# Band attention on Trainium2: the softmax sums in three pieces, and PSUM banks handed out by a list

## The chip, the cores and the metric

The kernel runs on one core of a Trainium2 chip. The metric is the device time of one execution in microseconds (us), as the median of several runs; smaller is better. TensorE (PE in the profile) multiplies, with PEld as its weight loads, VectorE is DVE, ScalarE is ACT, GpSimd is POOL and the sync engine, which issues the transfers, is SP. PSUM is the memory that PE writes to, eight banks of 512 fp32 columns on 128 partitions; DVE and ACT read it, POOL does not here.

## What is computed

One block of a model on x of shape (2, 256, 128, 128): batch, time, frequency band, channel. It has three residual steps: attention over time with a causal mask, attention over the bands with a band mask, and a feed-forward layer. Each is fed by a layer norm. There are 4 heads of 32 channels.

```python
cm, bm = _causal_mask(256), _band_mask(128, 16)      # bm: |i - j| <= 16
xt = _ln(x).transpose(0, 2, 1, 3)
x = x + _mha(xt, t_wi, t_bi, t_wo, t_bo, 4, cm).transpose(0, 2, 1, 3)
x = x + _mha(_ln(x), f_wi, f_bi, f_wo, f_bo, 4, bm)
x = x + gelu(_ln(x) @ w1.T + b1) @ w2.T + b2

# in _mha, per head
scores = q @ k.T / sqrt(32) + mask
o = softmax(scores) @ v
```

The change concerns the second attention. A sequence has 128 bands, and a query sees only the keys that are at most 16 bands away. A query among the first 48 bands therefore sees keys of the first 64 alone, one among the last 48 sees keys of the last 64 alone, and only the 32 queries in the middle see keys of both halves.

## The kernel before, in words

The work is cut into groups of four sequences (512 tokens). There are 128 groups over time, then sixteen **runs**, each of eight groups over bands (class `OverBands`) and eight groups of the feed-forward layer on the same tokens. The loop in `run` makes one pass, here called an iteration n, per group, and does in it the scores of group n, the softmax and value product of group n-1, the output product of group n-2 and the projections of group n+1. Within a run the iterations of the band groups are called n = 0 to 7 here, and n = 8 is the first of the feed-forward groups.

Every engine works in the order in which this loop writes its instructions (class `InOrder` pins it). An instruction that waits holds back everything behind it on its engine. In a steady iteration of the bands the engines do this:

- **PE**: scores of n (32 products on tiles of 32 rows by 64 columns); the softmax sums of n-1; values by weights of n-1; output product of n-2; query, key and value projections of n+1. The sums are four products, one per head, of a matrix of ones with the weights `pf` (keys on the 128 rows, 512 queries as columns), so that each of a head's 32 output rows holds the sum of that head.
- **ACT**: four exponentials of n (`pf<-bank`); the reciprocal of the sums of n-1 as a logarithm (`ln<-bank`) and an exponential (`r<-ln`); the copies of query, key and value projections of n+1 (`qT`, `kT`, `v`).
- **DVE**: limit and mask of the last head's scores in place (`bank<-bank,band`), called the clamp here; layer norm and turning for group n+3 (four `xh`, one `z`); residual sum of n-2 (`x<-bank,x`); one step that refines the reciprocal of n-1 (`bank<-bank,r`, then `u<-bank,r`) and the division (`oT<-bank,u`). In the iterations 3, 4, 5 and 7 of a run, statistics of a later layer norm follow (`stats`, `mv`).
- **POOL**: for the iterations that follow statistics, the root of the variance (`rstd`), then the band mask on the weights of the first three heads of n (six `pf<-pf`).

A PSUM bank is a tile of the pool `ps`, and bank numbers are handed out in the order in which the loop asks, one after the other, modulo eight (`turn_of_bank`). `OverBands.weigh` asks ahead for the banks of the output product and the query projection (`path.held`, `follow`). In the part over time the banks are named by hand (`place`, `banks`). A product that writes a bank waits until the last reader of what stood there is done.

The profile gives all recorded operations one line, that of the helper, so groups are told apart by tile names; a PSUM tile is called `bank` throughout. An fp32 product of PE makes two records in the trace.

Of the kernel before, what the change touches and what calls it, by code (L numbers as in the profile page):

```python
# [34 lines left out]
LARGE = 1e20  # L35
EXP_SET = "natural_log_exp_and_others"
# [327 lines left out]

def by_tile(t):

    return t.rearrange("p (i t q) -> p i t q", i=NT, q=D)


class Group:  # L370
# [7 lines left out]
    def __init__(self, path, src, dst, before=None, store=None):  # L378
        self.path, self.src, self.dst = path, src, dst
        self.before, self.store = before, store  # L380

# [179 lines left out]
class Attention(Group):  # L561
    which = None
    swapped = ()
# [7 lines left out]
    def queries_keys(self):  # L571
        path = self.path
        wf = path.k.wf[self.which]
        self.qp = path.bank([P, NT * P], "qp", self.place.get("qp", path.held.pop("qp", None)))
        product(path, self.qp, wf[:, 0:P], self.xnT)

        self.kp = path.bank([P, NT * P], "kp", self.place.get("kp"))
        product(path, self.kp, wf[:, P : 2 * P], self.xnT)

    def take_query(self):  # L580
        path = self.path
        self.qT = path.work.tile([P, NT * P], F32, name="qT")
        path.scalar.activation(self.qT, self.qp, AF.Identity, bias=path.k.bq[self.which], scale=1.0)

    def take_key(self):
        path = self.path
        self.kT = path.work.tile([P, NT * P], F32, name="kT")
        path.scalar.copy(self.kT, self.kp)

    def values(self):  # L590
        path = self.path
        wv = path.k.wf[self.which][:, 2 * P : 3 * P]
        self.vp = path.bank([P, NT, P], "vp", self.place.get("vp"))
        for i in range(NT):
            product(path, self.vp[:, i], self.xnT[:, i * P : (i + 1) * P], wv, turn=2 if i in self.swapped else 0)

    def take_values(self):
        path = self.path
        self.v = path.work.tile([P, NT, P], F32, name="v", bufs=4)
        path.scalar.copy(self.v, self.vp)  # L600

# [13 lines left out]
    def divide(self):  # L615

        path, vector = self.path, self.path.vector
        if self.r0 is None:
            self.oT = path.work.tile([P, NT * P], F32, name="oT", bufs=2)
            u = path.work.tile([P, NT * P], F32, name="u", bufs=2)  # L620
            vector.tensor_tensor(by_rows(u), by_tile(self.op), by_tile(self.r), ALU.mult)
            vector.tensor_scalar(self.oT, u, -1.0, None, ALU.mult)
            return
        vector.tensor_tensor(self.rp, self.rp, self.r0, ALU.mult)
        u = path.work.tile([P, NT * P], F32, name="u", bufs=2)
        vector.scalar_tensor_tensor(u, self.rp, 2.0, self.r0, ALU.subtract, ALU.mult)
        self.oT = path.work.tile([P, NT * P], F32, name="oT", bufs=2)
        vector.tensor_tensor(by_rows(self.oT), by_tile(self.op), by_tile(u), ALU.mult)

    def output(self):  # L630
        path = self.path
        self.yp = path.bank([P, NT, P], "yp", self.place.get("yp", path.held.pop("yp", None)))
        for i in range(NT):
            product(path, self.yp[:, i], self.oT[:, i * P : (i + 1) * P], path.k.wn[self.which])

    def finish(self):
        self.path.vector.tensor_tensor(self.dst(), self.yp, self.dst(), ALU.add)
        if self.store is not None:
            self.store()
# [13 lines left out]
class OverTime(Attention):  # L653
# [7 lines left out]
    def values(self):  # L661
        path = self.path
        wv = path.k.wf[self.which][:, 2 * P : 3 * P]
        self.vp = [path.bank([P, 2, P], "vp", self.place.get(f"vp{s}")) for s in range(2)]
        for i in range(NT):
            product(
                path, self.vp[i // 2][:, i % 2], self.xnT[:, i * P : (i + 1) * P], wv, turn=2 if i in self.swapped else 0
            )

    def take_values(self):  # L670
        path = self.path
        self.v = path.work.tile([P, NT, P], F32, name="v", bufs=4)
        for s in range(2):
            path.scalar.copy(self.v[:, 2 * s : 2 * s + 2], self.vp[s])

    def first_tiles(self):
# [3 lines left out]
        self.s0 = {h: path.bank([P, 2, 2 * P], "sp", path.banks[f"a{h}"]) for h in range(H)}  # L680

    def second_tiles(self):
# [3 lines left out]
        self.s1 = {h: path.bank([P, 2, P], "sp", path.banks[f"b{h}"]) for h in range(H)}  # L686
# [15 lines left out]
    def first_weights(self, heads):  # L702
        for h in heads:
            self.path.scalar.activation(self.p0[:, :, h], self.s0[h], AF.Exp)

    def second_weights(self, heads):
        for h in heads:
            self.path.scalar.activation(self.p1[:, :, h, 0], self.s1[h], AF.Exp)

# [17 lines left out]
    def weigh(self):  # L727
        path, v = self.path, self.v
        rp = path.bank([P, 2, 2, P], "rp", self.place.get("rp"))
# [4 lines left out]
        op = path.bank([P, 2, 2 * P], "op", self.place.get("op"))  # L734
# [33 lines left out]
class OverBands(Attention):  # L768
# [3 lines left out]
    follow = ("yp",)  # L772
    by_vector = 1

    def scores(self, heads):
        path = self.path
        self.sp = {h: path.bank([P, NT * P], "sp") for h in heads}
# [12 lines left out]
    def first_function(self):  # L790
# [6 lines left out]
        for h in range(H):  # L797
            path.scalar.activation(self.p[:, h].rearrange("p i q -> p (i q)"), self.sp[h], AF.Exp)

# [13 lines left out]

    def weigh(self):
        path = self.path

        path.held = {name: path.turn_of_bank() for name in self.follow}
        self.rp = path.bank([P, NT * P], "rp")
        for h in range(H):
            path.tensor.matmul(  # L820
                self.rp[rows_of(h), :], path.k.ones[:, 0:D], self.p[:, h].rearrange("p i q -> p (i q)"),
                start=True, stop=True,
            )
        self.op = path.bank([P, NT * P], "op")
# [7 lines left out]
class FeedForward(Group):  # L832
# [8 lines left out]
    def hidden(self, js):  # L841
        path = self.path
        for j in js:
            self.hp[j] = path.bank([P, NT * P], "hp")
            product(path, self.hp[j], path.k.w1f[:, j * P : (j + 1) * P], self.xnT)

    def gelus(self, js):
        path = self.path
        for j in js:
# [3 lines left out]
            )  # L853

# [14 lines left out]
    def weigh(self):  # L869
        path, NI = self.path, self.path.k.NI  # L870
        if self.last:
            zp = [path.bank([P, P], "zp") for i in range(NT)]
        else:
            self.zp = path.bank([P, NT, P], "zp")
# [11 lines left out]
    def divide(self):  # L886
# [5 lines left out]
        else:  # L892
            self.path.vector.tensor_tensor(self.dst(), self.zp, self.dst(), ALU.add)
        self.store()
# [17 lines left out]
class BoundedPath:  # L912
    def __init__(self, ctx, tc, k):
# [6 lines left out]
        self.next_bank = 0  # L920
        self.inputs = 0
        self.held = {}
# [20 lines left out]
    def turn_of_bank(self):  # L943
        i, self.next_bank = self.next_bank, (self.next_bank + 1) % 8
        return i

    def bank(self, shape, name, i=None):

        flat = self.ps[self.turn_of_bank() if i is None else i][:, 0 : math.prod(shape[1:])]
# [224 lines left out]
    def verdict(self):  # L1174

        vector, C = self.vector, P
        tp = self.bank([P, 6], "tp")
# [97 lines left out]
    def run(self, x, out):  # L1275
# [15 lines left out]
        for i in range(len(groups) - 2):  # L1291
            if at(i, OverBands) and at(i + 1, OverBands):
                groups[i].follow = ("yp", "qp")

# [18 lines left out]
        for n in range(len(groups) + 2):  # L1313
# [6 lines left out]
            if n + 4 in early:  # L1320
                do(n + 4, "root")
            do(n, "first_half", "first_function", "first_mask")
# [73 lines left out]
            if not bands[2] and not turn:  # L1396
                statistics_of_feed(n)
            do(n - 1, "weigh")
# [26 lines left out]
            do_at(n + 1, OverBands, "queries_keys", "take_query", "take_key")  # L1425
# [15 lines left out]
            do_at(n + 1, OverBands, "values", "take_values")  # L1441
            if old is not None or new is not None:
# [70 lines left out]
```

## Time and profile before

| | before |
|---|---|
| median of 3 runs | 2633.57 us (2630.35 to 2633.73) |
| span of the profiled execution, first to last instruction | 2631.9 us |
| TensorE clock granted | 1.000 |
| PE busy | 2617.8 us, 99% |
| PE weight loads | 1837.4 us, 70% |
| DVE busy | 2140.8 us, 81% |
| ACT busy | 1838.8 us, 70% |
| POOL busy | 1958.6 us, 74% |

The span of the profiled execution lies 1.7 us under the median of the runs. The share of busy time is a mean over three different parts (time, bands, feed-forward). [...]

### The profile page before, as it was taken

The numbers are of one execution on the slowest core, as the hardware profiler recorded it, in microseconds if no ns is written. First come the engines' busy times: TensorE is split into PE (matmuls) and PEld (weight loads), VectorE is DVE, ScalarE is ACT, GpSimd is POOL, SyncE is SP. The second block draws the span as 40 slices with busy tenths as digits, with TensorE's granted clock in tenths as the row PEclk, the third lists the DMA queues.
The fourth block names the chain that finished last, engine by engine and source line by source line (L and its number), as shares of the span: only waits on it lengthen the run. The fifth ranks groups of instructions, "written<-read, shape, count | busy, mean of one in ns | idle before, by whom it ended". The sixth has DMA issues, their size and how long they took to land.

```text
span 2631.9 us, 156460 instructions
## 1 busy us (share of the span) xinstructions
PE 2617.8 (99%) x68688; PEld 1837.4 (70%) x68688; DVE 2140.8 (81%) x6410; ACT 1838.8 (70%) x3543; POOL 1958.6 (74%) x2311
## 2 busy tenths in 40 slices
PE   9999999999999999999999999999999999999999
PEld 6666666666766767666777776667676677777776
DVE  8888888888888887977878779788797797887974
ACT  7989988999899875564655746647557466475573
POOL 7999999999999987666667666665776666757762
PEclk9999999999999999999999999999999999999999
DMA  6656555565565454445454544554454445554543
GB/s 155 167 149 158 149 149 149 155 155 149 149 158 149 122 127 119 115 123 127 118 124 124 123 122 117 126 128 120 122 126 120 120 119 131 123 120 123 123 104 88
DMA packets 469797, 344.97 MB, mean 131 GB/s; under 512 B 43120, under 2 KB 404464, under 8 KB 469104
## 3 DMA queue, kind: packets, MB, share of 16 engines
q1 hardware_dynamic: 468408, 334.41, 50.5%
q8 instruction: 540, 8.85, 1.5%
q14 instruction: 153, 1.25, 0.2%
q10 hardware_dynamic: 696, 0.46, 0.1%
HBM read 167.98 MB, written 166.72 MB: 127 GB/s over the span
## 4 chain that ended last, share of the span: by engine, by line
PE 99%; DVE 0%; issue 0%; DMA 0%; ACT 0%; ACTq 0%; DVEq 0%
PE bank L907 99%; DMA x<-in_x 0%; DVE xh L907 0%; DVE bank L907 0%; DVE res L907 0%; DVE stats L907 0%; DVE oT L907 0%; DVE u L907 0%; DVE xnT L907 0%; ACTq L907 0%; ACT p L907 0%; DVE vy L907 0%; ACT lnv L907 0%; DVE mv L907 0%; ACT root L907 0%
## 5 line engine op out<-in xcount | busy, mean ns | idle before, releaser
L907 ACT ACTIVATE hT<-bank,b 128x512 f32<-128x512 f32 x512 | 348.1, 688 | 524.2 <-PE bank L907 483.2
L907 POOL TENSOR_SCALAR_AFFINE_SELECT pf<-pf 128x512 f32<-128x512 f32 x768 | 477.7, 637 | 185.3 <-ACT pf L907 159.1
L907 PEld LDWEIGHTS bank<-w2T_sb,hT 128*32 128x32 f32 x16384 | 467.4, 110 | 54.8 <-issue 29.0
L907 PE MATMUL bank<-xnT,wf 128*32 128x512 f32 x4096 | 492.4, 592 | 0.5 <-DVE xnT L907 0.5
L907 PE MATMUL bank<-xnT,w1f 128*32 128x512 f32 x4096 | 486.3, 592 | 0.2 <-issue 0.2
L907 PE MATMUL bank<-w2T_sb,hT 128*32 128x128 f32 x16384 | 482.8, 273 | 1.0 <-issue 1.0
L907 ACT ACTIVATE p<-bank 128x512 f32<-128x512 f32 (+1 forms) x1024 | 430.6, 494 | 62.9 <-PE bank L907 62.9
L907 DVE TENSOR_SCALAR xh<-x,mv,rstd 128x160 f32<-128x160 f32 (+1 forms) x1012 | 394.3, 432 | 59.7 <-POOL rstd L907 49.4
L907 POOL TENSOR_SCALAR_AFFINE_SELECT p<-p 128x1024 f32<-128x1024 f32 (+2 forms) x384 | 364.5, 949 | 57.5 <-ACT p L907 49.1
L907 PEld LDWEIGHTS bank<-wf,xnT 128*32 128x32 f32 x8192 | 243.3, 110 | 144.1 <-issue 101.6
L907 POOL TENSOR_TENSOR p<-p,p 128x512 f32<-128x512 f32 x256 | 324.6, 1291 | 10.6
L907 DVE BATCH_NORM_STATS2 stats<-x 128x6 f32<-128x128 f32 x1536 | 329.0, 276 | 3.4 <-DMA x<-in_x 3.4
L907 POOL TENSOR_SCALAR rstd<-mv 128x4 f32<-128x4 f32 x251 | 57.8, 230 | 361.7 <-DVE mv L907 360.5
L907 PEld LDWEIGHTS bank<-xnT,w1f 128*32 128x32 f32 x4096 | 183.6, 110 | 171.6 <-issue 109.6
L907 PE MATMUL bank<-qT,kT 32*64 32x80 f32 (+4 forms) x16384 | 302.0, 271 | 0.1
L907 PEld LDWEIGHTS bank<-qT,kT 32*64 32x64 f32 x16384 | 260.0, 131 | 51.2 <-ACT kT L907 50.6
L907 DVE TENSOR_TENSOR res<-bank,res 128x512 f32<-128x512 f32 (+1 forms) x259 | 170.3, 658 | 153.3 <-PE bank L907 144.7
L907 ACT ACTIVATE pf<-bank 128x512 f32<-128x512 f32 x512 | 265.8, 602 | 35.5 <-PE bank L907 31.3
L907 PE MATMUL bank<-wn,oT 128*32 128x128 f32 x8192 | 283.8, 274 | 0.1
L907 DVE STREAM_TRANSPOSE z<-xh 128x512 f32<-128x512 f32 x380 | 270.3, 711 | 13.3
L907 PE MATMUL bank<-wf,xnT 128*32 128x128 f32 x8192 | 276.5, 273 | 0.0
L907 POOL TENSOR_TENSOR rstd<-rstd,mhalf 128x4 f32<-128x4 f32 x251 | 260.8, 1039 | 20.9
(100 smaller groups left out, 3820.3 us busy)
## 6 DMA issues: line engine op xcount, KB each, us to landing
turned<-z SPq DMA_DIRECT2D x1520, 64.0 KB, 2.7
xnT<-turned SPq DMA_DIRECT2D x380, 256.0 KB, 3.2
x<-res SPq DMA_DIRECT2D x256, 128.0 KB, 2.5
x<-x SPq DMA_DIRECT2D x128, 256.0 KB, 4.1
out<-res SPq DMA_DIRECT2D x252, 128.0 KB, 2.3
x<-in_x SPq DMA_DIRECT2D x124, 256.0 KB, 4.3
x<-in_x SPq DMA_DIRECT2D x4, 128.0 KB, 2.8
x<-in_x SPq DMA_DIRECT2D x6, 64.0 KB, 2.9
```

What stands on the lines that cost most here:

```text
L907: return self.tc.keep_in_program_order(emit(*args, **kwargs))
```

## The change

The sums of a band group are made in three pieces where both neighbours in the loop are band groups (seven of the eight groups of a run, 112 of 128):

- `outer_sums`, right behind the scores of the next group: queries 0 to 47 of each sequence by keys 0 to 63, and queries 80 to 127 by keys 64 to 127. These are eight products on tiles of 64 rows by 32 columns and 192 columns long. The two halves write two banks, `rp` and `lower`.
- then the query projection of group n+1 and its copy, which were further down;
- then `middle_sums`: queries 48 to 79 by all 128 keys, four products of 128 columns into `rp`, and the values by weights as before.

ACT's logarithm becomes two (columns 0 to 79 of each sequence from `rp`, 80 to 127 from `lower`), and DVE's first refining product becomes two, of which one reads `lower` and writes into `rp`. Banks are now handed out by a list: `take` removes the first free one, `give` appends it once the code has written its last reader, and the order of the list is that of the giving.

```diff
+    def outer_sums(self):
+
+        self.split = True
+        self.rp = self.take("rp", [P, NT * P])
+        self.lower = self.take("lower", [P, NT * EDGE])
+        for h in range(H):
+            self.sums_of(h, in_tiles(self.rp)[:, :, 0:EDGE], slice(0, EDGE), slice(0, HALF))
+            self.sums_of(h, in_tiles(self.lower), slice(P - EDGE, P), slice(HALF, P))
+
+    def middle_sums(self):
+        q = slice(EDGE, P - EDGE)
+        for h in range(H):
+            self.sums_of(h, in_tiles(self.rp)[:, :, q], q, slice(0, P))
+
+    def sums_of(self, h, to, q, rows):
+        self.path.tensor.matmul(
+            to[rows_of(h)], self.path.k.ones[rows, 0:D], self.p[rows, h, :, q],
+            start=True, stop=True, skip_group_check=True,
+        )
...
+        path.scalar.activation(in_tiles(ln)[:, :, 0 : P - EDGE], in_tiles(self.rp)[:, :, 0 : P - EDGE], AF.Ln)
+        path.scalar.activation(in_tiles(ln)[:, :, P - EDGE : P], in_tiles(self.lower), AF.Ln)
...
+        vector.tensor_tensor(rp[:, :, low], in_tiles(self.lower), r0[:, :, low], ALU.mult)
+        self.give("lower")
+        vector.tensor_tensor(rp[:, :, q], rp[:, :, q], r0[:, :, q], ALU.mult)
...
     def weigh(self):
         path = self.path
 
-        path.held = {name: path.turn_of_bank() for name in self.follow}
-        self.rp = path.bank([P, NT * P], "rp")
-        for h in range(H):
-            path.tensor.matmul(
-                self.rp[rows_of(h), :], path.k.ones[:, 0:D], self.p[:, h].rearrange("p i q -> p (i q)"),
-                start=True, stop=True,
-            )
-        self.op = path.bank([P, NT * P], "op")
+        if self.split:
+            self.middle_sums()
...
+        self.op = self.take("op", [P, NT * P])
...
+            if bands[1] and bands[2]:
+                do(n - 1, "outer_sums")
+            if bands[2] and bands[3]:
+                do(n + 1, "queries", "take_query")
             do(n - 1, "weigh")
             do(n - 1, "invert_exactly" if turn else "invert")
...
-            do_at(n + 1, OverBands, "queries_keys", "take_query", "take_key")
+            if bands[2] and bands[3]:
+                do(n + 1, "keys", "take_key")
+                do_at(n - 1, OverBands, "give_sums")
+            else:
+                do_at(n - 1, OverBands, "give_sums", "give_values")
+                do_at(n + 1, OverBands, "queries_keys", "take_query", "take_key")
```

How the instructions move is shown at three places of a steady iteration of the bands. The first is PE, behind the last scores product of the iteration. Before:

```order
L907 MATMUL bank_114<-pf,ones 32x512 [waits Pool_49] x3
L907 MATMUL bank_114<-pf,ones 32x512
L907 MATMUL bank_115<-pf,v 32x128 [waits Activation_49]
L907 MATMUL bank_115<-pf,v 32x128 x15
L907 MATMUL bank_112<-wn_241,oT 32x128 [waits DVE_49]
L907 MATMUL bank_112<-wn_241,oT 32x128 x15
L907 MATMUL bank_113<-xnT,wf_238 32x512 [waits DMAHW6_49]
```

With the change, from the same place to the value product:

```order
L999 MATMUL bank_111<-pf,ones 32x4x48 [waits Pool_49]
L999 MATMUL bank_109<-pf,ones 32x192 [waits DVE_49]
L999 MATMUL bank_111<-pf,ones 32x4x48 [waits Pool_49]
L999 MATMUL bank_109<-pf,ones 32x192
L999 MATMUL bank_111<-pf,ones 32x4x48 [waits Pool_49]
L999 MATMUL bank_109<-pf,ones 32x192
L999 MATMUL bank_111<-pf,ones 32x4x48
L999 MATMUL bank_109<-pf,ones 32x192
L999 MATMUL bank_114<-xnT,wf_238 32x512 [waits DMAHW6_49,Activation_49]
L999 MATMUL bank_114<-xnT,wf_238 32x512 x3
L999 MATMUL bank_111<-pf,ones 32x4x32 x4
L999 MATMUL bank_108<-pf,v 32x128 [waits DVE_49]
```

Four long products became eight short ones, four query products and four middle ones. The first product into `lower` (bank 109 here) now waits for DVE, whose `u<-bank,r` of the group before read the same bank as that group's `rp`.

The second place is DVE between the residual sum and the statistics of one iteration. Before:

```order
L907 TENSOR_TENSOR x_33598<-bank_110,x_33598 128x512 [waits PE_49]
L907 TENSOR_TENSOR bank_112<-bank_112,r_35893 128x512 [waits Activation_49]
L907 SCALAR_TENSOR_TENSOR u<-bank_112,r_35893 128x512 [waits DVE_49]
L907 TENSOR_TENSOR oT<-bank_113,u 128x4x4x32 [waits DVE_49]
L907 BN_STATS stats<-x_33598 128x6 x4
```

With the change:

```order
L999 TENSOR_TENSOR x_34028<-bank_115,x_34028 128x512 [waits PE_49,Activation_49]
L999 TENSOR_TENSOR bank_110<-bank_113,r_36734 128x4x48 [waits Activation_49]
L999 TENSOR_TENSOR bank_110<-bank_110,r_36734 128x4x80 [waits DVE_49]
L999 SCALAR_TENSOR_TENSOR u<-bank_110,r_36734 128x512 [waits DVE_49]
L999 TENSOR_TENSOR oT<-bank_108,u 128x4x4x32 [waits DVE_49]
```

One product became two, and the second waits for the first one's result, since both write the same bank.

The third place is ACT, from the exponential of the last head on. Before:

```order
L907 ACTIVATE pf<-bank_113 128x512 [waits DVE_49]
L907 ACTIVATE ln<-bank_108 128x512 [waits PE_49]
L907 ACTIVATE r_36189<-ln 128x512 [waits Activation_49]
L907 ACTIVATE qT<-bank_115,bq_283 128x512 [waits PE_49]
L907 COPY kT<-bank_110 128x512 [waits PE_49]
```

With the change:

```order
L999 ACTIVATE pf<-bank_112 128x512 [waits DVE_49]
L999 ACTIVATE qT<-bank_114,bq_283 128x512 [waits PE_49]
L999 ACTIVATE ln<-bank_110 128x4x80 [waits PE_49]
L999 ACTIVATE ln<-bank_113 128x4x48
L999 ACTIVATE r_36734<-ln 128x512 [waits Activation_49]
L999 COPY kT<-bank_109 128x512 [waits PE_49]
```

The copy of the queries now stands ahead of the reciprocal. The banks of the scores also change hands: in a steady iteration the four of them are those that were read last by the exponential of the last head, the copy of the queries, the residual sum and the product on `lower` of the iteration before.

116 lines of the change are left out of this document (88 added, 28 removed).

## The prediction

> **What bounds the kernel now.** I read the chain of waits first, then the stretch of one undisturbed run of band groups (2201 to 2266 us) in order of time on PE, DVE and ACT, then the groups by shape for prices.
>
> ```profile
> PE 99%; DVE 0%; issue 0%; DMA 0%; ACT 0%; ACTq 0%; DVEq 0%
> ```
>
> By the chain, PE sets the end everywhere, and less work on PE should be less time. The order of time on PE in iteration 5 of that run (start, length, records), with the scores of iterations 1 to 3 and the output product of the run's last band group:
>
> ```profile
> 2208.67 0.96 PE L907 MATMUL bank<-qT,kT 32*64 32x80 f32 x64
> 2214.02 0.97 PE L907 MATMUL bank<-qT,kT 32*64 32x80 f32 x64
> 2220.25 0.96 PE L907 MATMUL bank<-qT,kT 32*64 32x80 f32 x64
> ...
> 2232.71 0.97 PE L907 MATMUL bank<-qT,kT 32*64 32x80 f32 x64
> 2233.60 1.07 PE L907 MATMUL bank<-pf,ones 128*32 128x512 f32 x8
> 2234.49 1.06 PE L907 MATMUL bank<-pf,v 128*32 128x128 f32 x32
> 2235.36 1.06 PE L907 MATMUL bank<-wn,oT 128*32 128x128 f32 x32
> 2236.23 1.90 PE L907 MATMUL bank<-xnT,wf 128*32 128x512 f32 x16
> 2237.95 1.06 PE L907 MATMUL bank<-wf,xnT 128*32 128x128 f32 x32
> 2238.93 0.96 PE L907 MATMUL bank<-qT,kT 32*64 32x80 f32 x64
> ...
> 2261.92 1.14 PE L907 MATMUL bank<-wn,oT 128*32 128x128 f32 x30
> ```
>
> From start to start the iteration is 6.22 us without a gap: scores 0.89, sums 0.89, values 0.87, output 0.87, query and key 1.72, value projection 0.98. DVE in the same run, from the clamp of iteration 3 to that output product, and its busy time in most of that stretch:
>
> ```profile
> 2221.40 0.70 DVE L907 SCALAR_TENSOR_TENSOR bank<-bank,band 128x512 f32<-128x512 f32 x1 [0.63 <-PE bank L907]
> ...
> 2224.28 0.65 DVE L907 TENSOR_TENSOR x<-bank,x 128x512 f32<-128x512 f32 x1
> 2224.86 0.69 DVE L907 TENSOR_TENSOR bank<-bank,r 128x512 f32<-128x512 f32 x1
> 2225.58 0.69 DVE L907 SCALAR_TENSOR_TENSOR u<-bank,r 128x512 f32<-128x512 f32 x1
> 2226.31 0.69 DVE L907 TENSOR_TENSOR oT<-bank,u 128x512 f32<-128x512 f32 x1
> 2226.91 0.86 DVE L907 BATCH_NORM_STATS2 stats<-x 128x6 f32<-128x128 f32 x4
> ...
> 2227.97 0.67 DVE L907 SCALAR_TENSOR_TENSOR bank<-bank,band 128x512 f32<-128x512 f32 x1
> ...
> 2254.66 1.61 DVE L907 TENSOR_SCALAR xh<-x,mv,rstd 128x160 f32<-128x160 f32 x4 [1.48 <-POOL rstd L907]
> ...
> 2261.44 0.43 DVE L907 TENSOR_SCALAR oT<-u 128x512 f32<-128x512 f32 x1
> ```
>
> ```profile
> 2221.40:2252.00 30.60, 29.90 (x74) 1.00 0.52 129
> ```
>
> This is what the chain does not tell. I call the time from the first scores product to the clamp the lag: 2221.40 less 2220.25 is 1.15 us, its least, since the clamp waits for the scores there. An iteration with statistics then takes DVE 6.57 (2221.40 to 2227.97), more than PE's 6.23, and the lag grows. From 2221.40 to 2252.00 DVE is busy for 29.90 of 30.60 us. It then waits 1.48 for a root that POOL makes of its own last statistics, goes through the reciprocal, and ends the division of the run's last group at 2261.44 + 0.43 = 2261.87. PE starts the product of that division at 2261.92, 0.05 later. So from iteration 3 of a run to that product **two engines are level**: time saved on PE gains nothing there, and time added on DVE arrives at 2261.92 in full.
>
> **The change on PE.** Sixteen records of 512 columns take 1.72 us with four tiles side by side: 0.43 per record, 0.84 ns per column. The outer sums have 192 columns, 0.16 per record and two records a tile: 0.32 if all eight tiles run side by side. A change of tile shape costs the 0.11 by which the value projection, before the scores, is longer than the value product of equal records (0.98 against 0.87). One such change is new, from 64 rows to 128; with 0.05 for first weights (an estimate, half of that 0.11) the outer sums take 0.48. The middle ones are eight records of 128 columns, a quarter of 0.87: 0.22. With 0.03 for the query's first weights it is 0.73 against 0.89, so **0.15 less** an iteration.
>
> No row shows a tile of 64 rows. The nearest are the scores over time, 64 records in 1.31 us (402.55 to 403.86) with 160 columns on average, 0.134 each: 6.5 run side by side there.
>
> ```profile
> 402.55 1.39 PE L907 MATMUL bank<-qT,kT 32*64 32x64 f32 x64
> 403.86 1.08 PE L907 MATMUL bank<-wn,oT 128*32 128x128 f32 x32
> ```
>
> If four at a time ran, the outer sums would be 0.80 and the iteration 0.17 longer. I take 0.15 less, by that row.
>
> ```profile
> L907 PE MATMUL bank<-p,v 128*32 128x256 f32 x2048 | 158.3, 379 | 1.3 <-issue 1.3
> L907 PE MATMUL bank<-p,ones 128*32 128x256 f32 x2048 | 134.0, 379 | 0.0
> L907 ACT ACTIVATE p<-bank 128x512 f32<-128x512 f32 x512 | 292.2, 597 | 0.6 <-PE bank L907 0.6
> L907 ACT ACTIVATE p<-bank 128x256 f32<-128x256 f32 x512 | 183.6, 390 | 62.3 <-PE bank L907 62.3
> L907 DVE TENSOR_TENSOR bank<-bank,r 128x512 f32<-128x512 f32 x240 | 166.8, 695 | 102.1 <-PE bank L907 78.9 <-ACT r L907 23.2
> L907 DVE TENSOR_TENSOR res<-bank,res 128x128 f32<-128x128 f32 x4 | 1.1, 291 | 3.7 <-PE bank L907 3.7
> ```
>
> The new sums write PSUM in runs of 48 and 32 columns. The time part's sums (`p,ones`) write two runs of 128 and take 379 ns, as long as `p,v`, which writes 256 columns in one run. The Trainium skill, page "PSUM — Partial Sum Buffer", section "Specifications (TRN2)", says that any non-contiguous access slows matmuls significantly; at runs of 128 this trace does not agree, and for shorter runs no row here shows it. I charge nothing in the sum and keep it as a rival.
>
> **The change on ACT and DVE.** ACT's price is 0.81 ns a column (207 ns for 256), so the logarithm's pieces of 320 and 192 columns are 0.44 and 0.34 long. An exponential passes on after 0.48 (row of four below, 1.93), 0.11 before its end: 0.33 + 0.37 against the 0.66 of one, **+0.04**. DVE's is 1.05 ns a column (695 against 291): pieces of 0.36 and 0.49. Each next one needs the one before, which costs 0.03 beyond the length (2224.86 to 2225.58 is 0.72 for 0.69). That is 0.39 + 0.52 against 0.72: **+0.19** for each split group. If the second piece did not wait for the first it would start 0.07 before its end (the residual sum, 0.65, passes on after 0.58): +0.09. With the fixed part of 0.16 and both waits in full it is +0.22. I take 0.19, since the order has the second piece wait.
>
> **Up to iteration 3.** ACT in iteration 1, with the refining step on DVE behind it:
>
> ```profile
> 2209.68 2.07 ACT L907 ACTIVATE pf<-bank 128x512 f32<-128x512 f32 x4 [0.29 <-PE bank L907]
> 2211.61 0.63 ACT L907 ACTIVATE ln<-bank 128x512 f32<-128x512 f32 x1
> 2212.27 0.63 ACT L907 ACTIVATE r<-ln 128x512 f32<-128x512 f32 x1
> 2212.80 0.67 ACT L907 ACTIVATE qT<-bank,bq 128x512 f32<-128x512 f32 x1
> 2213.38 0.57 ACT L907 COPY kT<-bank 128x512 f32<-128x512 f32 x1
> ...
> 2212.93 0.70 DVE L907 TENSOR_TENSOR bank<-bank,r 128x512 f32<-128x512 f32 x1 [0.16 <-ACT r L907]
> ```
>
> ACT runs through and ends `kT` at 2213.95, just before the scores at 2214.02, so ACT already sets iteration 1 (5.35), and PE's 0.15 is worth nothing in it; the split logarithm makes it 5.39. With the copy of the queries ahead, the reciprocal ends 0.58 + 0.04 later, and DVE, which waited for it (0.16), starts its product 4.88 us after the scores, not 4.26. Its `u` ends at 4.88 + 0.39 + 0.52 + 0.69 = 6.48. Behind it the first product into `lower` waits, and everything on PE behind that; PE would be there at 5.39 + 0.90 = 6.29. With 0.06 for the signal (estimate, near the 0.05 above) it loses 0.25, so iteration 2 is 6.23 - 0.15 + 0.25 = 6.33. **Scores of iteration 3: 0.14 later.**
>
> The lag: with the query product between, the output product ends, and with it the residual sum can start, at 0.90 + 0.48 + 0.89 + 0.22 + 0.87 + 1.06 + 0.10 = 4.52 after the scores (DVE comes there at 1.15 + 2.88 = 4.03 now, 2221.40 to 2224.28). In iteration 2 it is 4.77 with the stall. From there to the next clamp are 0.58 + 0.91 + 0.73 + 0.60 = 2.82, which gives 7.59 less 6.33: lag 1.26 at iteration 3, **0.11 more**. There DVE reaches the residual sum at 1.26 + 2.88 = 4.14 and waits to 4.52: **0.38 more**. After that the lag is so long that this wait is gone.
>
> **The sum.** Iterations 3 to 7 each hold one split product: 5 x 0.19 = 0.95. 0.14 + 0.11 + 0.38 + 0.95 = 1.58 us a run arrive at the run's last output product; sixteen runs give 25. PE pauses for instructions now and then, as in the first row, after which DVE's clamp waits for PE again (the second, two iterations on):
>
> ```profile
> 1599.81 0.64 PE L907 MATMUL bank<-pf,v 128*32 128x128 f32 x16 [0.30 <-issue]
> ...
> 1611.23 0.70 DVE L907 SCALAR_TENSOR_TENSOR bank<-bank,band 128x512 f32<-128x512 f32 x1 [0.33 <-PE bank L907]
> ```
>
> All its idle time is 14 us (2631.9 less 2617.8). Where DVE leads, such pauses cost nothing more; I estimate a fifth, 3 us, saved. So +22: 2631.9 becomes 2654, and with the 1.7 by which the median lies above the profile, **2655 us**. Where the wait shows: scores of n+1 need the bank that the product on `lower` reads, lag + 2.88 + 0.58 + 0.36 + 0.06 after the scores of n. That makes iterations of about 6.1, 6.2, 6.8 and 6.8 from 3 on, with lags of 2.3, 2.9, 2.9 and 1.8 (6.2 before). POOL's masks, which follow a root of DVE's statistics, are late by the same lag, and the first three heads' outer sums can wait for them too.
>
> **The rivals.**
>
> *The outer sums are slow* (tiles four at a time, or short runs in PSUM; the page's rule is this case). 0.32 more in iteration 2, in the wait of iteration 3 and some 0.1 in iteration 1: 0.75 a run more, 12 us, 2667. The row of 6.5 side by side speaks against the first, nothing against the second. Chance 0.13.
>
> *DVE's pieces are nearly free and the early waits hide in the lag.* 5 x 0.09 less the 3 us: +4, 2638. For it: DVE's rows overlap by 0.07 where none depends on another; against: the order has them wait. Chance 0.15.
>
> *PE is the bound after all, and it is faster.* In the run around 1600 us a pause let DVE catch up, and the clamp's wait of 0.33 shows PE leading there; if that holds for all, 0.15 in each of seven iterations and sixteen runs is 17 us: 2617. It decides from the point where DVE's additions in a run stay below its idle time there (0.7 of 30.6 us). I add twice as much. Chance 0.12.
>
> That the change does less than it says I exclude: the order shows 112 split groups with these shapes.
>
> **Numbers.** Forecast 0.60, rivals 0.13, 0.15 and 0.12. A measurement here tells about 0.2% (5 us) from no change. Faster 0.12; the second rival within 5 us and its edge, 0.14; slower 0.74. The range runs from 2634, just below the second rival, to 2672, above the first.
>
> **What would show it.** Right: in the profile after, scores starts 6.6 to 6.9 apart in iterations 5 and 6 of a run, lags above 2, DVE without idle time from iteration 3 to the last `oT`, two DVE pieces taking 0.9 together, `lower` waiting for DVE in iteration 2. Wrong: iterations of 6.1 throughout, a lag that returns to 1.15, or outer sums far from 0.48 from start to start.

## The result, and the profile after

The changed kernel takes 2668.85 us in the median (2664.89 to 2673.35, four runs) against 2632.64 of the kernel before (2630.35 to 2633.73, four runs). The ratio is 1.0138, with a 95% interval of 1.0125 to 1.0150: **36 us slower**. Forecast were 2655, in a range of 2634 to 2672.

The profiled execution of the changed kernel is 2673.35 us with a span of 2671.3, so it is the longest of the four, 39 us over the span before. Its chain of waits, as shares of the span by engine, is no longer PE alone:

```profile
PE 82%; DVE 11%; DMA 2%; ACT 2%; issue 2%; POOL 1%; SPq 1%; ACTq 0%; DVEq 0%; POOLq 0%
```

The order of time on PE in one run of band groups, that which starts at 1797 us (start, length, records): scores of iterations 1 to 3, iteration 4 in full, scores of 5 to 7, and the output product of the run's last group. The records overlap (1.06 long, the next 0.87 later), so stretches are counted from start to start.

```profile
1804.19 0.97 PE L999 MATMUL bank<-qT,kT 32*64 32x80 f32 x64
1809.58 0.97 PE L999 MATMUL bank<-qT,kT 32*64 32x80 f32 x64
...
1815.94 0.97 PE L999 MATMUL bank<-qT,kT 32*64 32x80 f32 x64
...
1822.02 0.97 PE L999 MATMUL bank<-qT,kT 32*64 32x80 f32 x64
1822.91 0.56 PE L999 MATMUL bank<-pf,ones 64*32 64x192 f32 x16
1823.40 1.06 PE L999 MATMUL bank<-xnT,wf 128*32 128x512 f32 x8
1824.28 0.40 PE L999 MATMUL bank<-pf,ones 128*32 128x128 f32 x8
1824.50 1.06 PE L999 MATMUL bank<-pf,v 128*32 128x128 f32 x32
1825.37 1.06 PE L999 MATMUL bank<-wn,oT 128*32 128x128 f32 x32
1826.24 1.04 PE L999 MATMUL bank<-xnT,wf 128*32 128x512 f32 x8
1827.10 1.06 PE L999 MATMUL bank<-wf,xnT 128*32 128x128 f32 x32
1828.09 1.07 PE L999 MATMUL bank<-qT,kT 32*64 32x80 f32 x64
...
1835.05 0.97 PE L999 MATMUL bank<-qT,kT 32*64 32x80 f32 x64
...
1841.80 0.97 PE L999 MATMUL bank<-qT,kT 32*64 32x80 f32 x64
...
1859.37 0.86 PE L999 MATMUL bank<-wn,oT 128*32 128x128 f32 x24
```

From start to start the outer sums take 0.49 (1822.91 to 1823.40), the middle ones 0.22, and the iteration 6.07 (to the next scores at 1828.09) where it took 6.22. The iterations from 1 on are 5.39, 6.36, 6.08, 6.07, 6.96 and 6.75. DVE in the same run:

```profile
1817.28 0.69 DVE L999 SCALAR_TENSOR_TENSOR bank<-bank,band 128x512 f32<-128x512 f32 x1
...
1820.49 0.69 DVE L999 TENSOR_TENSOR x<-bank,x 128x512 f32<-128x512 f32 x1 [0.27 <-PE bank L999]
1821.10 0.89 DVE L999 TENSOR_TENSOR bank<-bank,r 128x192 f32<-128x192 f32 x2
1822.02 0.69 DVE L999 SCALAR_TENSOR_TENSOR u<-bank,r 128x512 f32<-128x512 f32 x1
1822.75 0.69 DVE L999 TENSOR_TENSOR oT<-bank,u 128x512 f32<-128x512 f32 x1
...
1824.41 0.67 DVE L999 SCALAR_TENSOR_TENSOR bank<-bank,band 128x512 f32<-128x512 f32 x1
...
1831.15 0.67 DVE L999 SCALAR_TENSOR_TENSOR bank<-bank,band 128x512 f32<-128x512 f32 x1
...
1858.89 0.43 DVE L999 TENSOR_SCALAR oT<-u 128x512 f32<-128x512 f32 x1
```

The two pieces with the step to `u` take 0.92 (1821.10 to 1822.02). The lag grows from 1.34 (1817.28 less 1815.94) to 2.39 and 3.06 (1831.15 less 1828.09). The last division ends at 1859.32, and PE starts its output product at 1859.37, again 0.05 later: the two engines are level there, and DVE arrives late. Over all sixteen runs the median of each iteration, from the scores of iteration 1 to those of 7, sums to 37.6 us, against 36.6 before, and from the scores of iteration 7 to the next run's first scores the median is 62.5 against 61.9. So **a typical run is 1.6 us longer, 26 us for sixteen**.

That leaves some 10 us of the 36, and 13 of the 39 in the profiled execution. The means lie above those medians by far more than before, because single iterations take 7.3 to 8.2 us. What ends PE's waits, in all, times and longest (the first row is of the kernel before, the others of the changed one):

```profile
PE bank L907 <- issue: 4.4, 9, 1.3
```

```profile
PE bank L999 <- issue: 17.9, 20, 1.8
DVE x L999 <- PE bank L999: 17.1, 28, 2.1
```

"issue" means that PE waits for nothing that the profile shows: no semaphore, no buffer. The trace also holds the packets of the queue that brings instructions (packets, MB), first before, then after:

```profile
q8 instruction: 540, 8.85, 1.5%
```

```profile
q8 instruction: 555, 9.09, 1.5%
```

A packet is 16384 bytes. PE has 68688 product records and as many weight loads before, 70480 after: in both kernels that is 254 of them to a packet. Read against these packets, the long pauses have one form. Times from the trace of the changed kernel, in us; the length is the step from the product record before to the next one, less the usual step there:

```
pause ends   length   last packet starts   and has landed
 1297.08      1.63        1294.18            1295.58
 2040.05      1.91        2037.40            2038.65
 2142.82      1.50        2140.15            2141.37
 2258.84      1.73        2256.16            2257.46
```

PE goes on 1.4 to 1.5 us after a packet of instructions has landed. In the stretch from the first band group on, the profile has 13 waits on issue over 0.5 us. All 13 end between 1.2 and 1.55 us after a landing, though packets come only every 4.8 us. All pauses over 0.2 us that end 1.15 to 1.65 after a landing sum to some 21 us after and 4 to 5 before; the exact sum depends on what is taken for the usual step. Two theories follow. **"Chain alone"**: the loss is the longer chain on DVE and ACT and the waits for banks, as the prediction had it. **"Instructions late"**: on top of it, the sixteen more product records and sixteen more weight loads of each split group make PE run out of instructions.

### The profile page after: what moved, and what is told of

Its sections match the earlier page's. It is cut to its first block, busy times and chain, and to the rows that moved or that the text cites. A ratio compares the mean times of both kernels' runs of the same rounds, so it can differ in the third digit from the quotient of the medians.

```text
span 2671.3 us, 160423 instructions
## 1 busy us (share of the span) xinstructions
PE 2636.4 (99%) x70480; PEld 1801.2 (67%) x70480; DVE 2160.1 (81%) x6522; ACT 1841.3 (69%) x3655; POOL 1958.2 (73%) x2311
## 3 DMA queue, kind: packets, MB, share of 16 engines
q14 instruction: 155, 1.27, 0.2%
## 4 chain that ended last, share of the span: by engine, by line
PE 82%; DVE 11%; DMA 2%; ACT 2%; issue 2%; POOL 1%; SPq 1%; ACTq 0%; DVEq 0%; POOLq 0%
PE bank L999 82%; DVE xh L999 2%; DVE bank L999 2%; DVE ln L999 1%; DVE u L999 1%; DVE x L999 1%; DVE oT L999 1%; DMA xnT<-turned 1%; ACT pf L999 1%; DVE stats L999 1%; DMA turned<-z 1%; DVE z L999 1%; SPq L999 1%; POOL rstd L999 0%; DVE mv L999 0%
## 5 line engine op out<-in xcount | busy, mean ns | idle before, releaser
L999 PE MATMUL bank<-xnT,wf 128*32 128x512 f32 x4096 | 517.8, 595 | 3.1 <-issue 1.3
L999 PEld LDWEIGHTS bank<-w2T_sb,hT 128*32 128x32 f32 x16384 | 456.3, 110 | 75.0 <-issue 50.0
L999 PE MATMUL bank<-xnT,w1f 128*32 128x512 f32 x4096 | 471.9, 593 | 2.1 <-DVE ok L999 2.1
L999 PE MATMUL bank<-w2T_sb,hT 128*32 128x128 f32 x16384 | 473.3, 273 | 0.2 <-issue 0.2
L999 PE MATMUL bank<-qT,kT 32*64 32x80 f32 (+4 forms) x16384 | 307.8, 272 | 11.7 <-issue 10.2
L999 PE MATMUL bank<-wn,oT 128*32 128x128 f32 x8192 | 278.4, 274 | 2.2 <-DVE oT L999 2.0
L999 DVE TENSOR_TENSOR bank<-bank,r 128x192 f32<-128x192 f32 (+1 forms) x352 | 185.4, 527 | 115.4 <-PE bank L999 80.8
L999 PEld LDWEIGHTS bank<-xnT,w1f 128*32 128x32 f32 x4096 | 139.8, 110 | 204.5 <-issue 175.5
```

Source lines behind the costliest of these rows:

```text
L999: return self.tc.keep_in_program_order(emit(*args, **kwargs))
```

## The experiments

All are compared with the kernel before on the same chip, whose median was 2635.4 to 2636.6 there. "Records" are PE product records; each product makes two.

**Queries ahead of the outer sums.** The two edited lines of the loop change places:

```diff
-            if bands[1] and bands[2]:
-                do(n - 1, "outer_sums")
             if bands[2] and bands[3]:
                 do(n + 1, "queries", "take_query")
+            if bands[1] and bands[2]:
+                do(n - 1, "outer_sums")
```

> The changed kernel with the query product ahead of the outer sums instead of behind them; every instruction and bank count as in the change. Theory 'instructions late': the extra pauses of the PE in the changed kernel (20.7 us in 26 pauses that each end 1.2 to 1.6 us after a packet of instructions has landed, against 4.2 us in 9 before) come from 32 value records, 64 scores records and 16 outer records in one stretch of some 2.25 us; the 8 long records of the query product now part scores and outer sums, so the pauses go back to some 4 to 8 us, and the wait for the lower bank in the second iteration of a run (0.14 us, 16 times) goes too: 2669 - 13 - 2 = about 2654. Theory 'chain alone': all the loss is the longer VectorE and ScalarE chain behind the sums and the bank waits; the middle sums end at the same time as before the swap, so only the lower bank's 2 us go: about 2667. A third possibility: the outer sums, now next to the middle ones, end later for the first half of Ln, which nothing uses earlier: no change.

Measured: 2676.15, ratio 1.0159 (1.0145 to 1.0174). It is no better than the change, and both theories missed; the third possibility, no change, comes closest. Pauses behind packets came to 13 to 15 us, fewer than the change's 21 but far from the expected 4 to 8, and they still stood in the scores. In return PE's weight loads wait longer for POOL's masks than in the change (8.3 us in 31 waits there):

```profile
PEld bank L999 <- POOL pf L999: 23.8, 37, 1.8
```

So the place of one long product between two dense stretches does not cure it. My picture of a stretch of 2.25 us at the scores was too narrow.

**Sums by tile in the kernel before.** More records, nothing else:

```diff
-        for h in range(H):
-            path.tensor.matmul(
-                self.rp[rows_of(h), :], path.k.ones[:, 0:D], self.p[:, h].rearrange("p i q -> p (i q)"),
-                start=True, stop=True,
-            )
+        for i in range(NT):
+            for h in range(H):
+                path.tensor.matmul(
+                    self.rp[rows_of(h), i * P : (i + 1) * P], path.k.ones[:, 0:D], self.p[:, h, i, :],
+                    start=True, stop=True,
+                )
```

> The kernel before with the sums of a group written as 16 products of 128 columns instead of 4 of 512: the same columns streamed, 32 records instead of 8 behind the 64 of the scores, nothing else moved. Theory 'instructions late': values, scores and sums are now 128 records in 2.65 us where they were 104; pauses behind instruction packets grow from 4 us to between 12 and 40 us, and the time from 2633 to between 2641 and 2670. Theory 'chain alone': the same columns, the same banks, the same waits: 2631 to 2636.

Measured: 2669.65, ratio 1.0133 (1.0117 to 1.0148). **As much as the whole change, with no change of tile shape, bank, order, ACT or DVE.** The products themselves stream as before: the undisturbed iteration is 6.24 against 6.23. But few iterations are undisturbed: the median of iterations 2 to 6 is 6.68 against 6.23. The waits on issue that the profile counts grow from 4.4 us:

```profile
PE bank L908 <- issue: 18.8, 40, 1.2
```

That is 14 of the 33 us. Counted as above, from start to start and behind a packet, the pauses over 0.2 us are some 28 us here, 23 more than before. Where the other 10 lie is not resolved.

**The dose.** The same kernel with 12 products of 256, 128 and 128 columns (24 records, exactly the number of the change) and with 8 of 256 (16 records):

```diff
-        for h in range(H):
-            path.tensor.matmul(
-                self.rp[rows_of(h), :], path.k.ones[:, 0:D], self.p[:, h].rearrange("p i q -> p (i q)"),
-                start=True, stop=True,
-            )
+        for c in (slice(0, 2 * P), slice(2 * P, 3 * P), slice(3 * P, 4 * P)):
+            for h in range(H):
+                path.tensor.matmul(
+                    self.rp[rows_of(h), c], path.k.ones[:, 0:D],
+                    self.p[:, h].rearrange("p i q -> p (i q)")[:, c], start=True, stop=True,
+                )
```

> The kernel before with the sums of a group as 12 products of 256, 128 and 128 columns: 24 records where it has 8, exactly as many records as the change adds to an iteration, and nothing else of the change. With 32 records the same kernel came to 2670. Theory 'instructions late' (the PE runs out of instructions; what counts is records per time): 16/24 of that 33 us, about 2655 (2648 to 2662), with PE waits on issue of 10 us or more. If it is a matter of 32 records in a row alone, or of products over 128 columns streaming slower: 2634 to 2640, or the same 2670.

> The kernel before with the sums as 8 products of 256 columns: 16 records, 8 more than it has, where 16 more cost 21 us and 24 more 34. Theory 'instructions late', in proportion: +9 to +12, 2644 to 2648; if there is a point below which nothing waits, between 2634 and 2641.

Measured: 2656.14, ratio 1.0072 (1.0059 to 1.0086), and 2642.70, ratio 1.0026 (1.0015 to 1.0036). Waits on issue in the two, 24 and 16 records:

```profile
PE bank L908 <- issue: 17.8, 33, 1.7
```

```profile
PE bank L908 <- issue: 5.3, 15, 0.9
```

With 8, 16 and 24 more records than the kernel before, the loss is 7, 21 and 33 us. That is 0.9, 1.3 and 1.4 us for each record added to an iteration. The 24 records came out as expected. The 16 fell between the two ranges: less than in proportion, and not nothing.

**Keys by tile in the kernel before.** As many more records as with sums by tile, but far from the scores:

```diff
-        product(path, self.kp, wf[:, P : 2 * P], self.xnT)
+        pieces = 4 if self.which == 1 else 1
+        w = NT * P // pieces
+        for c in range(pieces):
+            product(path, self.kp[:, c * w : (c + 1) * w], wf[:, P : 2 * P], self.xnT[:, c * w : (c + 1) * w])
```

> The kernel before with the key product of the band groups as 16 products of 128 columns instead of 4 of 512: 24 records more in an iteration, as many as in the kernel with sums by tile (+33 us), but between the output and the values, as far from the scores as the iteration has a place, and no instruction of the sums is touched. If what counts is how many instructions the PE takes in an iteration: +20 to +35, 2655 to 2670. If only the stretch at the scores and the sums counts: 2634 to 2642.

Measured: 2663.97, ratio 1.0119 (1.0104 to 1.0135), 29 us more than before.

```profile
PE bank L910 <- issue: 18.1, 26, 1.8
```

In this kernel, too, all 15 waits on issue over 0.5 us end 1.15 to 1.65 us after a landing; with sums by tile it is 15 of 16, with 24 records 12 of 12. That stretch behind the landings holds about a tenth of the time. What counts is therefore how many instructions PE takes in an iteration of 6.2 us, and hardly where they stand. It fits that the queries moved ahead of the outer sums were no help.

**The list alone.** The loop's calls of `outer_sums`, of the early `queries` and `take_query`, and the condition on the keys are taken out, so the sums stay whole and only the hand-out of banks is new:

```diff
-            if bands[1] and bands[2]:
-                do(n - 1, "outer_sums")
-            if bands[2] and bands[3]:
-                do(n + 1, "queries", "take_query")
...
+            do_at(n - 1, OverBands, "give_sums", "give_values")
+            do_at(n + 1, OverBands, "queries_keys", "take_query", "take_key")
```

> The changed kernel with banks by the list but the sums whole and the queries beside the keys as before. Both theories: no change within 0.2% (2630 to 2637); what the list itself can cost is the wait of about 2.3 us, once, at the first product behind the tests. If it is over 2640, part of the loss lies in the banks.

Measured: 2644.83, ratio 1.0037 (1.0023 to 1.0050): 8 us, where I had put nothing but the one wait of 2.3. In iteration 2 of each run one of the banks that the scores take is that which DVE's `u` of the group before still reads, and the scores take 1.27 to start of sums where they took 0.89. In order of time, DVE, PE, and the weight loads that resume:

```profile
1900.82 0.69 DVE L999 SCALAR_TENSOR_TENSOR u<-bank,r 128x512 f32<-128x512 f32 x1
...
1901.18 1.30 PE L999 MATMUL bank<-qT,kT 32*64 32x80 f32 x64
...
1901.56 0.76 PEld L999 LDWEIGHTS bank<-qT,kT 32*64 32x64 f32 x58 [0.19 <-DVE u L999]
```

0.38 in sixteen runs is 6 us, and the wait behind the tests, 2.0, is the rest. The changed kernel has the same wait in the same iteration; there it is the product on `lower` that stands behind `u`.

**The order alone.** The list, the query product ahead of the whole sums, and nothing in pieces:

```diff
-            if bands[1] and bands[2]:
-                do(n - 1, "outer_sums")
```

> The list and the query product ahead of the whole sums, Ln and VectorE undivided: the order alone, with no record added. Terms of the prediction for what is late by one query product (residual sum 0.38, clamp 0.11 in a run) on the list's 2645, less the list's own wait for the scores' bank (6 us) if the new order takes it away: 2645 to 2653. If moving the queries costs nothing at all: 2637 to 2645.

Measured: 2651.33, ratio 1.0061 (1.0048 to 1.0075), 16 us over before. PE also waits 4.3 us (6 times) for the transfer of `xnT`, the input of the query product, which it now needs earlier; with the list alone that is 0.4, and the prediction had no term for it. The changed kernel shows no such wait. The residual sum `x` waits for the later output product, as the prediction said it would; the row of this kernel, and behind it that of the next experiment, which leaves the queries where they were:

```profile
DVE x L999 <- PE bank L999: 20.4, 32, 2.2
```

```profile
DVE x L997 <- PE bank L997: 0.9, 2, 0.5
```

**The pieces alone.** List and old order, whole sums on PE, but Ln and DVE's product in two pieces:

```diff
-    self.lower = self.take("lower", [P, NT * EDGE])
+    self.lower = in_tiles(self.rp)[:, :, P - EDGE : P]
...
-        if self.split:
-            self.middle_sums()
+        for h in range(H):
+            path.tensor.matmul(
+                self.rp[rows_of(h), :], path.k.ones[:, 0:D], self.p[:, h].rearrange("p i q -> p (i q)"),
+                start=True, stop=True,
+            )
```

> The list and the old order with whole sums on the PE, but Ln and the VectorE product in two pieces each, as in the change. The list alone came to 2645 (the bank wait of the third iteration of a run, 0.38 us x 16, and 2.3 us once). Term of the prediction: five pieces of 0.19 us in a run delay the clamps and so the pace, 0.95 us x 16 = 15: 2660. Rival: the longer VectorE queue is hidden, since the PE of the old order is slower by 0.15 us in each iteration and gives VectorE that time: 2645 to 2650.

Measured: 2663.78, ratio 1.0103 (1.0089 to 1.0118): 19 us over the list alone, by the medians, where the term said 15 and the rival nothing to 5. DVE's pieces are not hidden. Some 3.5 of the 19 stand where the term had none: in iteration 2 the scores wait for `u`, which the pieces make later, and its median is 6.83 against 6.61 with the list alone.

**The sums split, the queries not moved.**

```diff
-            if bands[2] and bands[3]:
-                do(n + 1, "queries", "take_query")
...
+            do_at(n + 1, OverBands, "queries_keys", "take_query", "take_key")
```

> The changed kernel with the split sums but the query product back beside the keys (outer and middle sums follow each other). The terms of the later sums, of the lower bank and of the residual sum (0.14 + 0.11 + 0.38 us in a run) fall away, the 0.95 us of five divided VectorE products stays. Theory 'chain alone': 2633 + 16 x 0.95 = about 2648. Theory 'instructions late': no long product stands any more between scores, outer, middle and weighted values (152 records in 3.3 us with the values product ahead), so the pauses are at least those of the change: 2648 + 16 to 30 = 2664 to 2678.

Measured: 2673.79, ratio 1.0142 (1.0126 to 1.0157), inside what "instructions late" expected and far from 2648. It has the list and the pieces, as the experiment above, and besides only the split sums on PE, with a bank of their own for the lower half. These cost another 9 to 10 us (1.0142 against 1.0103), although each makes its iteration shorter on PE (the shortest here is 6.07).

**Both kernels without the refinement.** The division in the band groups is one VectorE product instead of three operations; the minus sign goes into the copy of the values. What is left out is the refining step of the reciprocal.

```diff
+        if self.which == 1:
+            self.oT = path.work.tile([P, NT * P], F32, name="oT", bufs=2)
+            vector.tensor_tensor(by_rows(self.oT), by_tile(self.op), by_tile(self.r0), ALU.mult)
+            self.give("rp", "lower", "op")
+            return
         self.multiply()
...
-        path.scalar.copy(self.v, self.vp)
+        path.scalar.activation(self.v, self.vp, AF.Copy, scale=-1.0 if self.which == 1 else 1.0)
```

> The kernel before without the refinement of the reciprocal in the band groups (two of VectorE's three operations of the division left out, 1.4 us a group; the sign goes into the copy of the values): a foot for the next kernel. The lags of the clamps fall to 1.15 in all iterations; the PE is the bound either way, so little moves: 2620 to 2634, 2629 likeliest.

> The changed kernel without the refinement, so that no divided VectorE product, no late residual sum and no bank wait for u is left; Ln stays in two pieces. To be read against the kernel before without the refinement. Theory 'chain alone': what is left is the PE's saving of 0.15 us in some six iterations of a run, 16 times: 14 us less than that kernel. Theory 'instructions late': the 16 to 17 us of pauses stay, since the records stay: 0 to 5 us more than that kernel, with iterations of 6.07 where no pause falls and 7 to 8 where one does.

Measured: the kernel before without the refinement 2629.90, ratio 0.9980 (0.9970 to 0.9989); the changed one without it 2646.41, ratio 1.0039 (1.0026 to 1.0052). So with the whole DVE term gone **the change still costs 16 us**, where "chain alone" expected a gain of 14. "Instructions late" had the sign and was too low with 0 to 5. The kernel before without it came out as expected (2620 to 2634). The scores' starts in a run without a pause (PE in order of time, first, second and last of six):

```profile
2335.86 0.97 PE L1004 MATMUL bank<-qT,kT 32*64 32x80 f32 x64
2341.94 0.97 PE L1004 MATMUL bank<-qT,kT 32*64 32x80 f32 x64
...
2366.24 0.97 PE L1004 MATMUL bank<-qT,kT 32*64 32x80 f32 x64
```

Five iterations in 30.38 us, 6.08 each where the other kernel takes 6.23: here is the saving on PE, in full. And here is what takes it away, in the next run:

```profile
2447.63 0.97 PE L1004 MATMUL bank<-qT,kT 32*64 32x80 f32 x64
2448.52 0.35 PE L1004 MATMUL bank<-pf,ones 64*32 64x192 f32 x1
2450.65 0.89 PE L1004 MATMUL bank<-pf,ones 64*32 64x192 f32 x15 [1.78 <-issue]
2451.47 1.93 PE L1004 MATMUL bank<-xnT,wf 128*32 128x512 f32 x8
2453.18 0.65 PE L1004 MATMUL bank<-pf,ones 128*32 128x128 f32 x8
...
2457.32 0.97 PE L1004 MATMUL bank<-qT,kT 32*64 32x80 f32 x64
```

After the first of the outer sums PE waits 1.78 us for nothing, and goes on 1.23 after a packet that landed at 2449.42. This iteration is 9.69 long. Waits on issue in the whole of this kernel, and in the kernel before without the refinement:

```profile
PE bank L1004 <- issue: 19.8, 24, 2.4
```

```profile
PE bank L911 <- issue: 1.1, 4, 0.4
```

A run that no pause disturbs (for each place in the run, the time that a fifth of the runs 2 to 15 stay below, summed) is 104.4 us against 105.2, 13 us less in sixteen runs. So all that disturbs the runs costs 29 more here than in the other kernel. Pauses behind packets are 22 to 24 us of it in the profiled execution (2 in the other kernel). PE also waits 2.6 us for `xnT`, as with the order alone (0.4 in the other kernel), and runs twice at half clock for 3.4 us, as shown at the end. The list and the new order are still in this kernel, so the 29 are not the price of the records alone, and I have not resolved the rest.

## Why the prediction was right, and where it failed

The direction was right, the time lies in the range, and the typical run came out as worked out: 1.6 us longer, as forecast (1.58). That the range also holds the 14 us beyond the forecast of 2655 is luck: its upper edge was set by slow outer sums, which did not come. Step by step:

- **PE's saving of 0.15** (0.89 less its 0.73 is 0.16): right. 0.49 for the outer sums (0.48), 0.22 for the middle ones, 6.07 for the iteration, and 6.08 throughout once DVE is out of the way.
- **Iteration 1 set by ACT, 5.39**: right, 5.39.
- **Iteration 2 by the wait on `u`, 6.33**: 6.36. The cause is shared with the list: without any split the same bank costs 0.38 there. My expectation of a free list was wrong by these 6 us; the prediction's sum held the wait, as one of the split.
- **Lag at iteration 3 of 1.26, and a residual sum 0.38 late**: 1.34 and 0.27. The order alone shows that wait without any piece (20.4 us against 0.9).
- **DVE's pieces, 0.91 with `u` and 0.19 more a group, with iterations of 6.1, 6.2, 6.8, 6.8 and lags of 2.3, 2.9, 2.9, 1.8**: 0.92; in the run shown 6.08, 6.07, 6.96, 6.75, and over all runs median lags of 2.40, 3.01, 2.84 and 1.78. The pieces alone cost 19 us for the 15 charged.
- **Two engines level at the run's last output product**: right, 0.05 apart in both kernels.

**The step that failed is the pauses.** The prediction saw that "PE pauses for instructions now and then" and made of it a gain: 3 us saved where DVE leads. It asked who absorbs the pauses and not what makes them. The change adds sixteen product records and as many weight loads to an iteration of 184 records, and the pauses behind instruction packets went from some 4 to some 21 us. Part of that is absorbed where DVE leads, as the prediction had it. The rest makes, with the once-only wait behind the tests (2.1, and an estimated 1.7, half of 3.41, for the half clock that follows it), the 10 us between the typical runs' 26 and the 36 measured. The parts tried alone agree: list and pieces 28, order 8 beyond the list, records 18, less 17 saved on PE, is 37.

The rivals: *outer sums slow* gave 2667, closest to the time, but by a mechanism that is not there. They take 0.49, half of them in runs of 48 columns in PSUM, and the middle ones, in runs of 32, take 0.22. The Trainium skill, page "PSUM — Partial Sum Buffer", section "Specifications (TRN2)", has non-contiguous access slow matmuls significantly; at these runs the trace does not agree. *DVE's pieces nearly free* falls with the pieces alone. *PE is the bound after all* is the instructive one: with the refinement gone PE is the bound, and the change is still slower, by 16 us. The rival's 17 us of gain (0.15 in 112 iterations) are no more than what 16 records cost in the kernel before (21 us in 128 groups, so 18 in 112). **The change does not win here even on a free VectorE.** No version tried with the change in it beats the kernel before; leaving the refinement out of the kernel before gains 0.2%, which is another edit.

Still open: what decides which packets bring a pause, and what makes up the rest of the 29 us in the unrefined kernel. That the pauses are a late supply of instructions is read from their place behind the packets and from the dose; no run changes the supply itself.

## What to carry to other kernels

Before cutting a product into shorter ones, count instructions per time and not only columns: here a PE stream of some 30 records and as many weight loads per us was at the edge, and each further record in an iteration cost about as much as was saved by streaming less. Look in the waits for "issue" on an engine that waits for nothing, and hold it against the packets of the instruction queue; a kernel that shows a few such pauses may have little room left, as this one had. To learn the price of an edit's instructions apart from its work, add as many to the old kernel without changing what they compute.

## What the runs showed of the hardware

**Instructions have a supply, and it can run out.** That was not expected at this size. The Trainium skill, page "Runtime: NRT & Kernel Launch", section "Instruction fetch mechanics", says that instructions come in blocks of 16 KiB, 256 instructions, and that crossing a block is mostly hidden. The size agrees with the packets here (16384 bytes, 254 PE records each). That it is hidden held in the kernel before (4.4 us of waits on issue in 2632) and no longer with 24 more records in an iteration (18.8 us in the waits, 33 us in the time).

**A pause of some 2 us can halve PE's clock for 3.4 us.** In the unrefined changed kernel two pauses, of 2.0 and 1.8 us, are followed by stretches of half the granted clock of 3.41 us each; a third, of 2.4 us at 1181 us, is not. Windows behind that at 2450 and that at 1181 (busy time of PE, PEld, DVE, ACT, POOL with instructions, granted clock, DMA share, GB/s):

```profile
1181.00:1185.00 4.00, 3.67 (x102) 2.68 (x105) 2.89 (x6) 2.40 (x5) 3.01 (x5) 1.00 0.32 80
2450.00:2454.00 4.00, 3.35 (x43) 1.37 (x46) 1.60 (x4) 1.23 (x3) 3.09 (x5) 0.57 0.30 73
```

The query product at 2451.47, in such a stretch, takes 1.71 to the next start instead of 0.88. The changed kernel has one such stretch, at 1022.8, behind a wait that the list brings in: the product after the tests takes the bank at the list's head, which DVE's `ok` still reads.

```profile
1018.97 0.39 PE L999 MATMUL bank<-tests,ones 128*128 128x6 f32 x2
1021.47 2.42 PE L999 MATMUL bank<-xnT,w1f 128*32 128x512 f32 x16 [2.12 <-DVE ok L999]
```

The Trainium skill, page "TensorE: Matmul & The Clock Gate", section "What's actually happening", names an activity window of about 3.4 us that runs freely, and half rate after an idle one. The length and the halving agree. Here a pause of about 2 us was enough, though not each time: six stretches of 3.41 us in the kernels shown, two in the unrefined one and four behind the wait at the tests (the change, the order alone, the pieces alone and the sums not moved). With the list alone and with the queries first, the same wait of 2.0 and 2.1 us was not followed by one.
